# A graph-network layer on one core: B's rows for two tiles in one transfer

## The chip, the cores and the metric

The kernel runs on one core of a Trainium2 chip. The core has five engines that run side by side, each with a queue of its own: PE (matrix multiply), DVE (vector), ACT (scalar), POOL (which issues the indirect gathers here) and SP (which issues most of the other transfers). The transfers themselves are carried by 16 DMA engines. The metric is the device time of one execution in microseconds (us). Times are compared as medians over several executions.

## The reference

A graph has N = 12500 nodes with 64 features `x` and E = 200000 edges, each with a source `src`, a destination `dst` and 32 features. The edges come sorted by destination. The destinations are not spread evenly: they are 12500 times the square of a uniform number, so low nodes have many edges and high nodes few.

```python
msg_in = concatenate([x[src], x[dst], edge], -1)          # 64 + 64 + 32
messages = relu(msg_in @ mW1 + mb1) @ mW2 + mb2           # hidden size 128
aggregated = segment_sum(messages, dst, N)
update = relu(concatenate([x, aggregated], -1) @ uW1 + ub1) @ uW2 + ub2
out = layernorm(x + update)
```

## The kernel before

The first product is split into three: A = x @ mW1[:64] and B = x @ mW1[64:128] + mb1 are computed once per node and written to tables in HBM (`tab_a`, `tab_b`, rows of 128 floats, 512 bytes), and the edge features give the third part.

The edges are cut into 1563 tiles of 128 (`P`). Eight tiles (`SUB`) make a group, the unit of the main loop, which runs over 196 groups `s`; two groups make a supergroup `g` of 16 tiles (`SUP`), 98 in all. Per tile:

- POOL gathers the 128 rows of A that the sources name, with one indirect transfer (`gather`, line 166). Eight tiles go to one row buffer `xg`; there are 14 such buffers (`ROWB`), so POOL can be up to 14 groups ahead and then has to wait until the addition that reads a buffer is done. The first eight groups gather rows of x and not of A.
- The rows of B for the destinations are not gathered. As the edges are sorted, the 128 destinations of a tile lie in a range of 32 nodes (`WIN`), which begins at the tile's first destination. `windows` (lines 217 to 227) loads these 32 rows of B for each tile with one transfer on SP's queue; the first row's number is a value that SP loads into a register (line 222, one load for the eight tiles of a group). The destination is `rhs`, two buffers of one supergroup each.
- `l` holds what multiplies these rows: 32 partitions with the edge features (transposed, loaded by `load`, line 213), and 32 partitions that first receive the destinations' numbers (`loadd`, line 182, each number repeated on 32 partitions) and then, after a comparison on DVE (`select`, lines 192 and 194), a 0/1 selection matrix. An even tile has partitions 0 to 63, the next odd one 64 to 127; in each half the edge features come first (`EK` = 0), then the selection (`SK` = 32). `rhs` has the same layout: the weights mW1[128:] beside the edge features, the window of B beside the selection. There are three buffers for `l`.
- `edge_part` (line 253) multiplies `l` by `rhs` for the tile: B's row for each edge plus the edge features' part. `node_part` adds the gathered A row on DVE (line 274) and applies the rectifier on ACT (line 275).
- `collect` multiplies the result by a second 0/1 matrix `sel`, tile by 32 (line 198, from `drc`, the distance of each destination from the start of its range), and adds the sum into an accumulator of 480 columns, at an offset that PE loads into a register from `woff` (line 300; line 305 counts the edges).

The accumulator covers one of 34 periods of nodes; at a period's end `close`, `update`, `residual`, `norm` and `store` finish its nodes, and `columns` loads x for them on SP's queue (line 328).

The order of the work is written out by hand. In each turn `s` of the main loop it is: gathers as far as buffers allow; `windows(s + 2)`; `node_part(s)`; `collect(s - 1)`; in even turns `select(g + 1)`, `load(g + 1)`; in odd turns `loadd(g + 2)`; parts of the table B while it is still being computed; `edge_part(s + 1)`; and the end of a period where one is due. SP's queue thus has, for two groups, 16 windows with two register loads, two loads of edge features and two of destinations, one after the other.

A check on the device (`checks`) tests that all destinations lie within their ranges and otherwise runs a general, slow version. With this data it doesn't run, before or after.

Of the kernel before, what the change touches and what calls it, by code (L numbers as in the profile page):

```python
# [32 lines left out]
EBULK = TPP * P * P  # L33
PADDST = -100000
PADWIN = 1000000
EK, SK = 0, DE
ROWB = 14
XG = 8
NCH = 8
# [1 line left out]
EARLY = NCH * P  # L41
GE = 20
# [1 line left out]
UB = 4  # L44
NCOL = (-(-N // P) + UB) * P
UN = 448
UW = UN + WIN
ONE = D - 1


# [12 lines left out]
UPD = updates()  # L63


@with_exitstack
def gnn_kernel(ctx: ExitStack, tc: tile.TileContext, x1T, x, eT, e_rows, src, dst, dst_row, wrow, wnext, whalf,
               mW1, mb1, mW2, mb2, uW1, ub1, uW2, ub2, out):

# [22 lines left out]
    nc = tc.nc  # L92
    const = ctx.enter_context(tc.tile_pool(name="const", bufs=1))
# [8 lines left out]

    src_s = const.tile([P, NT], I32, name="src_s")
    wint = const.tile([1, NTP], I32, name="wint")
    past = const.tile([1, 1], F32, name="past")
# [22 lines left out]
    pidx = const.tile([P, 1], F32, name="pidx")  # L128
    one = const.tile([P, 1], BF, name="one")
    zero_b = const.tile([P, UW], BF, name="zero_b")  # L130

# [3 lines left out]
    drc = const.tile([P, NT], F32, name="drc")  # L135
# [4 lines left out]
    wh = const.tile([P, NTP // 2], I32, name="wh")  # L140
# [11 lines left out]
    def tiles(s):  # L152
        return range(s * SUB, min((s + 1) * SUB, NT))
# [17 lines left out]
    with tc.tile_pool(name="sup", bufs=2) as sup, tc.tile_pool(name="work", bufs=2) as work, tc.manual_schedule():  # L171
        L, S, SB, xs, hs, pcs, sums = {}, {}, {}, {}, {}, {}, {}
        pt = psum.tile([P, SUB // 2, P], F32, name="pt", tag="sums")

        def loadd(g):

            l = operand[g % 3]
            o = g * SUP * P
            dv = dst_row[:, o:o + SUP * P].rearrange("o (k b e) -> o b k e", b=2, e=P)
            for b in range(2):  # L180
                q = 64 * b + SK
                nc.sync.dma_start(l[q:q + WIN].bitcast(I32), dv[:, b].broadcast_to([WIN, SUP // 2, P]))
            L[g] = l

        def select(g):


            nt = min(SUP, NT - g * SUP)
            l = L[g]
            c = WIN + SUP // 2 * (g % 2)  # L190
            node = cps[:, c:c + SUP // 2]
            nc.vector.tensor_scalar(node, wh[:, g * SUP // 2:(g + 1) * SUP // 2], pidx, None, op0=ALU.add)
            for r in ([slice(0, P)] if g > 2 else [slice(SK, SK + WIN), slice(64 + SK, 64 + SK + WIN)]):
                nc.vector.tensor_tensor(l[r], l[r].bitcast(I32),  # L194
                                        node[r].unsqueeze(2).broadcast_to([r.stop - r.start, SUP // 2, P]),
                                        op=ALU.is_equal)
# [12 lines left out]
        def load(g):  # L209

            for b in range(2):
                q = 64 * b + EK
                nc.sync.dma_start(L[g][q:q + DE], eT[g, b])

        def windows(s):

            g = s // (SUP // SUB)
            o = s % (SUP // SUB) * SUB
            nt = len(tiles(s))
            r = rhs[g % 2]  # L220
            tab, n = (B0, EARLY - WIN + 1) if g < GE else (B, N)
            _, ws = nc.values_load_multi_w_load_instructions(
                wint[0:1, s * SUB:s * SUB + nt], engines=[ET.SP], min_val=0, max_val=n - 1,
                skip_runtime_bounds_check_because="destinations are node numbers")
            for i in range(nt):
                q = SK + 64 * (i % 2)
                nc.sync.dma_start(r[q:q + WIN, (o + i) // 2, :], tab[bass.ds(ws[i], WIN), :])

        def transpose(s):

# [142 lines left out]
        def relative(a, b):  # L373

            wbc = work.tile([P, WCH], I32, name="wbc", tag="tb")
            nc.sync.dma_start(dst_s[:, a:b], dst[:, a:b])
            nc.sync.dma_start(wbc[:, :b - a], wrow[:, a:b].broadcast_to([P, b - a]))
            nc.vector.tensor_tensor(drc[:, a:b], dst_s[:, a:b], wbc[:, :b - a], op=ALU.subtract)

        def halves(a, b):  # L380

            for h in range(2):
                nc.sync.dma_start(wh[64 * h:64 * h + 64, a:b], whalf[h:h + 1, a:b].broadcast_to([64, b - a]))


        Av, Bv, B0v = (t.rearrange("(c p) f -> p c f", p=P) for t in (A, B, B0))
# [44 lines left out]

        def offsets():

            nc.vector.memset(usup[:, 0:1], 0)
            wv = wint.rearrange("o (s t) -> o s t", t=SUB)
            ov = woff.rearrange("o (s t) -> o s t", t=SUB)
            k = 0
            while k < K:
                end = UPD[k + 1:] + [NSUB]
                d = end[0] - UPD[k]  # L440
                n = 1
                while k + n < K and k and end[n] - UPD[k + n] == d:
# [20 lines left out]
        nc.gpsimd.iota(pidx_i, pattern=[[0, 1]], base=-SK, channel_multiplier=1)  # L463
        nc.gpsimd.iota(pidx_i[64:], pattern=[[0, 1]], base=-SK, channel_multiplier=1)
        for s in range(XG):
            gather(s)
        nc.vector.tensor_copy(slot, slot_i)
        nc.vector.tensor_copy(pidx, pidx_i)
        nc.vector.memset(one, 1.0)
        nc.vector.memset(zero_b, 0.0)  # L470
        for t in (*xw, hT):
# [4 lines left out]
        nc.sync.dma_start(wint, wrow)  # L476
        halves(0, 4 * SUP)
        loadd(0)
        loadd(1)
        for r in rhs:  # L480
            for o in (EK, EK + 64):
                nc.sync.dma_start(r[o:o + DE], mW1[2 * D:, :].unsqueeze(1).broadcast_to([DE, SUP // 2, DH]))
        for k, c in enumerate(range(0, NB, NCH)):
            chunk_a(c)
            if k == 0:
                chunk_b(0, [B0v, Bv])
            if k == 2:

                w0 = wint[:, :GE * SUP]
                nc.vector.tensor_scalar(past, w0[:, GE * SUP - 1:], float(EARLY - WIN), None, op0=ALU.is_gt)  # L490
                nc.vector.tensor_scalar(w0, w0, float(EARLY - WIN), None, op0=ALU.min)
# [91 lines left out]
        for s in range(last + 3):  # L583
            g, j = divmod(s, SUP // SUB)
# [42 lines left out]
    with tc.If(flag > 0), tc.tile_pool(name="gen", bufs=1) as up:  # L627
# [28 lines left out]
        with tc.For_i(0, NT, 1) as t:  # L656
# [31 lines left out]
            h = up.tile([P, DH], F32, name="hg")  # L688
# [29 lines left out]
        with tc.For_i(0, NB, 1) as c:  # L718
# [24 lines left out]
            o = up.tile([P, D], F32, name="o")  # L743
# [45 lines left out]
```

## Time and profile before

| | |
|---|---|
| time, three executions | 2738.41, 2741.72, 2743.06 us (median 2741.72) |
| profiled execution | 2739.58 us, span of the core 2737.8 us |
| granted TensorE clock | 0.529 of full speed |
| busy share PE, DVE, ACT, POOL | 57%, 20%, 12%, 54% |
| window transfers (`rhs<-tab_b`) | 1563 on SP's queue, 16.0 KB each |
| loads of `l` | 196 of destinations, 196 of edge features, on SP's queue, 128.0 KB each as written |
| gathers of A (`xg<-tab_a`) | 1499 on POOL's queue, 128 rows each |
| bytes moved | 211.38 MB, 77 GB/s in the mean |

The busy shares are averages. SP has no busy share, as instructions that issue transfers or set registers aren't counted as busy; what SP does is read from its own records, its waits and its timeline. A row of a timeline gives the start, how long it lasted to the end of its last instruction, the engine (SPq is SP's queue), the line, the operation, what is written from what, and how many instructions were merged.

### The profile page before, as it was taken

What the parts mean: (1) busy time and instruction counts of PE and PEld (TensorE: products, weight loads), DVE (VectorE), ACT (ScalarE), POOL (GpSimd) and SP (SyncE); (2) the same over time, 40 slices, a digit from 0 to 9 for tenths busy, and PEclk for the clock granted to TensorE, in tenths of its full rate; (3) what the DMA queues carried; (4) which work ended last, traced back from release to release, by engine and by line L of the source; (5) the groups of instructions that cost most, each with busy time, mean ns of one, the idle gap of its engine ahead of it and who ended that gap; (6) DMA issues with size and microseconds to landing.
All of it is one profiled execution on the core that took longest, in us unless ns stands there. A gap on an engine that the chain in (4) does not pass through costs nothing. (4 is left out here: it accounts for less than half of the span.)

```text
span 2737.8 us, 34166 instructions
## 1 busy us (share of the span) xinstructions
PE 1572.4 (57%) x9254; PEld 1375.3 (50%) x9254; DVE 535.6 (20%) x1012; ACT 341.9 (12%) x454; POOL 1475.7 (54%) x1572
## 2 busy tenths in 40 slices
PE   1322755555655655636655565565675656576598
PEld 1311644444544545635545454455564545565477
DVE  0200121212211212212111221211221112121242
ACT  0100100101101111101111111111111111111122
POOL 7175455656566555555555555555555554655510
PEclk6555655555555555555555555555555555555555
DMA  3531233333222222222222222222222222222221
GB/s 90 143 93 52 77 85 91 96 91 92 77 77 72 72 74 76 80 66 75 73 70 74 72 75 75 76 75 73 72 76 73 70 71 73 75 75 75 73 75 39
DMA packets 242854, 211.38 MB, mean 77 GB/s; under 512 B 77245, under 2 KB 207935, under 8 KB 242672
## 3 DMA queue, kind: packets, MB, share of 16 engines
q0 software_dynamic: 50016, 100.44, 14.3%
q1 hardware_dynamic: 177102, 98.44, 12.9%
q10 hardware_dynamic: 15554, 10.31, 1.3%
q8 instruction: 87, 1.43, 0.2%
q14 instruction: 95, 0.78, 0.1%
HBM read 191.12 MB, written 17.83 MB: 76 GB/s over the span
## 5 line engine op out<-in xcount | busy, mean ns | idle before, releaser
L166 POOL DMA_INDIRECT xg<-tab_a,src_s x1499 | 1414.2, 943 | 1124.8 <-issue 419.2
L300 PEld LDWEIGHTS sums<-sel,h 128*128 128x128 f32 x3126 | 666.6, 308 | 394.1 <-issue 387.7
L300 PE MATMUL sums<-sel,h 128*128 128x32 f32 x3126 | 662.7, 369 | 343.2 <-issue 340.9
L253 PE MATMUL pc<-rhs,l 64*128 64x128 f32 x3126 | 509.9, 433 | 552.4 <-DMA l<-in_eT 277.7
L253 PEld LDWEIGHTS pc<-rhs,l 64*128 64x128 f32 x3126 | 416.6, 314 | 606.3 <-issue 559.4
L274 DVE TENSOR_TENSOR h<-pc,xg 128x1024 f32<-128x1024 f32 x189 | 229.0, 1212 | 985.7 <-issue 410.4
L275 ACT ACTIVATE h<-h 128x1024 f32<-128x1024 f32 x189 | 198.0, 1048 | 778.6 <-DVE h L274 624.9
L194 DVE TENSOR_TENSOR l<-l,cps 128x1024 f32<-128x1024 int32 (+1 forms) x101 | 123.4, 1221 | 252.4 <-DMA l<-in_dst_row 206.3
L198 DVE TENSOR_TENSOR sel<-cps,drc 128x512 f32<-128x512 f32 x98 | 67.2, 686 | 479.1 <-remote 204.1
L206 ACT CAST selb<-sel 128x512 bf16<-128x512 f32 x98 | 60.3, 616 | 560.7 <-DVE sel L198 220.3
L305 PE MATMUL cnt<-selb,one 128*1 128x32 bf16 x1563 | 85.2, 188 | 39.2 <-issue 36.9
L344 PE MATMUL py<-ux,xw 128*128 128x64 f32 x272 | 82.1, 398 | 11.2 <-issue 11.2
L408 PE MATMUL pb<-w1a,xl 64*128 64x128 f32 x196 | 29.8, 428 | 100.6 <-DMA xl<-in_x1T 57.2
L345 PE MATMUL py<-u,hTu 128*128 128x64 f32 x272 | 80.9, 392 | 11.0 <-issue 10.4
L305 PEld LDWEIGHTS <-one 128*1 128x1 bf16 x1563 | 56.1, 83 | 60.1 <-issue 49.0
L408 PEld LDWEIGHTS pb<-w1a,xl 64*128 64x128 f32 x196 | 25.4, 312 | 104.8 <-issue 87.4
L344 PEld LDWEIGHTS py<-ux,xw 128*128 128x128 f32 x272 | 67.7, 303 | 17.5 <-issue 16.7
L345 PEld LDWEIGHTS py<-u,hTu 128*128 128x128 f32 x272 | 68.9, 307 | 11.9 <-issue 11.2
L349 DVE BATCH_NORM_STATS2 st<-py 128x6 f32<-128x64 f32 x136 | 21.3, 219 | 269.4 <-PE py L345 147.6
L166 POOL DMA_INDIRECT xg<-in_x,src_s x64 | 60.5, 946 | 20.4 <-issue 19.2
L335 PE MATMUL pu<-sums_s,w2u 128*128 128x448 f32 x68 | 62.5, 1016 | 3.5 <-issue 3.1
L337 ACT ACTIVATE hTu<-pu,ub_s 128x448 f32<-128x448 f32 x34 | 21.5, 633 | 329.3 <-remote 155.8
(87 smaller groups left out, 474.9 us busy)
## 6 DMA issues: line engine op xcount, KB each, us to landing
l<-in_dst_row SPq DMA_DIRECT2D x196, 128.0 KB
l<-in_eT SPq DMA_DIRECT2D x196, 128.0 KB
rhs<-tab_b SPq DMA_DIRECT2D x1563, 16.0 KB
xg<-tab_a,src_s POOLq DMA_INDIRECT x1499
tab_b<-tb SPq DMA_DIRECT2D x13, 512.0 KB
tab_a<-tb ACTq DMA_DIRECT2D x12, 512.0 KB
out<-o SPq DMA_DIRECT2D x34, 128.0 KB
xw<-in_x1T SPq DMA_DIRECT2D x34, 113.8 KB
```

The lines of the kernel that those rows point to most:

```text
L166: nc.gpsimd.indirect_dma_start(out=a[:, i, :] if s < XG else a[:, i // 2, i % 2, :], out_offset=None, in_=A[:, :] if s >= XG else x[:, :], ...
L194: nc.vector.tensor_tensor(l[r], l[r].bitcast(I32), node[r].unsqueeze(2).broadcast_to([r.stop - r.start, SUP // 2, P]), op=ALU.is_equal)
L198: nc.vector.tensor_tensor(s[:, :nt], slot.unsqueeze(1).broadcast_to([P, nt, WIN]), drc[:, g * SUP:g * SUP + nt].unsqueeze(2).broadcast_to( ...
L206: nc.scalar.copy(sb[:, :nt], S[g][:, :nt])
L253: nc.tensor.matmul(pc[:, b, k, :], L[g][q:q + 64, m, :], rhs[g % 2][q:q + 64, m, :], start=s >= XG or k == 0, stop=s >= XG)
L274: nc.vector.tensor_tensor(hf[:, m], pf[:, m], a[:, m], op=ALU.add)
L275: nc.scalar.activation(hf[:, m], hf[:, m], AF.Relu)
L300: nc.tensor.matmul(ps[:, bass.ds(ws[i], WIN)], h[:, i % 2, i // 2, :], S[g][:, k0 + i, :], start=False, stop=ends and i == n - 1)
L305: nc.tensor.matmul(pn[:, bass.ds(ws[i], WIN)], one, SB[g][:, k0 + i, :], start=False, stop=ends and i == n - 1)
L335: nc.tensor.matmul(pu, w2u, sums_s[u % 2][:, :UN], start=True, stop=False)
L344: nc.tensor.matmul(py[:, i], xw[u % 2][:, i * P:(i + 1) * P], ux, start=True, stop=False)
L345: nc.tensor.matmul(py[:, i], hT[:, i * P:(i + 1) * P], u2, start=False, stop=True)
```

## The change

The ranges of an even tile and of the next odd one now lie a fixed distance apart: the even tile's range begins at its first destination, as before, and the odd tile's begins a constant number of nodes after that. The constant is 0 for the first 65 supergroups, where tiles are shorter in nodes, and then 2, 4, 6, 8 and 10 (`SHIFT`). Both ranges can so be read with one transfer, whose source is [2 halves, 32 rows, 128 floats] and whose destination is 64 adjacent partitions. For them to be adjacent, the odd tile's half has the selection first and the edge features last: `SK` = (32, 64), `EK` = (0, 96). `windows` issues 782 transfers of 64 rows where it issued 1563 of 32; the register load reads four values (`weven`) for a group, not eight.

What follows from it: `wint`, the start of every tile's range, is computed on DVE from `weven` (in `offsets`); the distances `drc` of odd tiles are corrected where the constant isn't 0; `pidx`, which turns partition numbers into node numbers, has one column for each constant; the accumulator gets 16 more columns (`UW` 480 to 496); `wh`, the even tile's first node on all partitions, is loaded in one transfer, not two.

```diff
-EK, SK = 0, DE
+EK, SK = (0, 96), (32, 64)
-UW = UN + WIN
+UW = UN + WIN + 16
...
+def shifts():
+    of = [2 * max(0, round(0.75 * (2.0 * N * P / E * (g + 1) * SUP * P / E - 10))) for g in range(NSUP)]
+    at = [g for g in range(NSUP) if g == 0 or of[g] != of[g - 1]]
+    return [(a, b, of[a]) for a, b in zip(at, at[1:] + [NSUP])]
...
         def windows(s):
             g = s // (SUP // SUB)
-            o = s % (SUP // SUB) * SUB
-            nt = len(tiles(s))
-            r = rhs[g % 2]
+            o = s % (SUP // SUB) * SUB // 2
+            nt = (len(tiles(s)) + 1) // 2
+            w = rhs[g % 2]
             tab, n = (B0, EARLY - WIN + 1) if g < GE else (B, N)
+            c = [c for a, b, c in SHIFT if a <= g < b][0]
+            pairs = bass.AP(tab.tensor, tab.offset, [[DH, tab.shape[0] - c], [c * DH, 2], [1, DH]])
             _, ws = nc.values_load_multi_w_load_instructions(
-                wint[0:1, s * SUB:s * SUB + nt], engines=[ET.SP], min_val=0, max_val=n - 1,
+                weven[0:1, s * SUB // 2:s * SUB // 2 + nt], engines=[ET.SP], min_val=0, max_val=n - 1,
                 skip_runtime_bounds_check_because="destinations are node numbers")
             for i in range(nt):
-                q = SK + 64 * (i % 2)
-                nc.sync.dma_start(r[q:q + WIN, (o + i) // 2, :], tab[bass.ds(ws[i], WIN), :])
+                nc.sync.dma_start(w[SK[0]:SK[0] + 2 * WIN, o + i, :],
+                                  pairs[bass.ds(ws[i], WIN)].rearrange("q h f -> h q f"))
...
             nc.vector.tensor_tensor(drc[:, a:b], dst_s[:, a:b], wbc[:, :b - a], op=ALU.subtract)
+            for g, h, c in SHIFT:
+                i, j = max(a, g * SUP) + 1, min(b, h * SUP)
+                if c and i < j:
+                    nc.vector.tensor_scalar(drc[:, i:j:2], drc[:, i:j:2], float(-c), None, op0=ALU.add)
...
         def halves(a, b):
-            for h in range(2):
-                nc.sync.dma_start(wh[64 * h:64 * h + 64, a:b], whalf[h:h + 1, a:b].broadcast_to([64, b - a]))
+            nc.sync.dma_start(wh[:, a:b], weven_row[:, a:b].broadcast_to([P, b - a]))
...
         def offsets():
+            wp = wint.rearrange("o (k b) -> o k b", b=2)
+            nc.vector.tensor_copy(wp[:, :, 0], weven)
+            for g, h, c in SHIFT:
+                g, h = g * SUP // 2, h * SUP // 2
+                nc.vector.tensor_scalar(wp[:, g:h, 1], weven[:, g:h], float(c), None, op0=ALU.add)
...
+        for k, (_, _, c) in enumerate(SHIFT):
+            nc.vector.tensor_copy(pidx[:, k:k + 1], pidx_i)
+            nc.vector.tensor_scalar(pidx[64:, k:k + 1], pidx[64:, k:k + 1], float(c), None, op0=ALU.add)
```

More of the change, by code (lines that the diff above doesn't have):

```diff
@@ L63, with gnn_kernel @@
 UPD = updates()
+def shifts():
+    of = [2 * max(0, round(0.75 * (2.0 * N * P / E * (g + 1) * SUP * P / E - 10))) for g in range(NSUP)]
+    at = [g for g in range(NSUP) if g == 0 or of[g] != of[g - 1]]
+    return [(a, b, of[a]) for a, b in zip(at, at[1:] + [NSUP])]
+SHIFT = shifts()
 @with_exitstack
-def gnn_kernel(ctx: ExitStack, tc: tile.TileContext, x1T, x, eT, e_rows, src, dst, dst_row, wrow, wnext, whalf,
+def gnn_kernel(ctx: ExitStack, tc: tile.TileContext, x1T, x, eT, e_rows, src, dst, dst_row, wrow, wnext, weven_row,
                mW1, mb1, mW2, mb2, uW1, ub1, uW2, ub2, out):
@@ L104, in gnn_kernel @@
     wint = const.tile([1, NTP], I32, name="wint")
+    weven = const.tile([1, NTP // 2], I32, name="weven")
     past = const.tile([1, 1], F32, name="past")
@@ L127, in gnn_kernel @@
     pidx_i = const.tile([P, 1], I32, name="pidx_i")
-    pidx = const.tile([P, 1], F32, name="pidx")
+    pidx = const.tile([P, len(SHIFT)], F32, name="pidx")
     one = const.tile([P, 1], BF, name="one")
@@ L180, in loadd @@
             for b in range(2):
-                q = 64 * b + SK
-                nc.sync.dma_start(l[q:q + WIN].bitcast(I32), dv[:, b].broadcast_to([WIN, SUP // 2, P]))
+                nc.sync.dma_start(l[SK[b]:SK[b] + WIN].bitcast(I32), dv[:, b].broadcast_to([WIN, SUP // 2, P]))
             L[g] = l
@@ L190, in select @@
             c = WIN + SUP // 2 * (g % 2)
+            k = [a <= g < b for a, b, _ in SHIFT].index(True)
             node = cps[:, c:c + SUP // 2]
-            nc.vector.tensor_scalar(node, wh[:, g * SUP // 2:(g + 1) * SUP // 2], pidx, None, op0=ALU.add)
-            for r in ([slice(0, P)] if g > 2 else [slice(SK, SK + WIN), slice(64 + SK, 64 + SK + WIN)]):
+            nc.vector.tensor_scalar(node, wh[:, g * SUP // 2:(g + 1) * SUP // 2], pidx[:, k:k + 1], None, op0=ALU.add)
+            for r in ([slice(0, P)] if g > 2 else [slice(q, q + WIN) for q in SK]):
                 nc.vector.tensor_tensor(l[r], l[r].bitcast(I32),
@@ L211, in load @@
             for b in range(2):
-                q = 64 * b + EK
-                nc.sync.dma_start(L[g][q:q + DE], eT[g, b])
+                nc.sync.dma_start(L[g][EK[b]:EK[b] + DE], eT[g, b])
         def windows(s):
             g = s // (SUP // SUB)
-            o = s % (SUP // SUB) * SUB
-            nt = len(tiles(s))
-            r = rhs[g % 2]
+            o = s % (SUP // SUB) * SUB // 2
+            nt = (len(tiles(s)) + 1) // 2
+            w = rhs[g % 2]
             tab, n = (B0, EARLY - WIN + 1) if g < GE else (B, N)
+            c = [c for a, b, c in SHIFT if a <= g < b][0]
+            pairs = bass.AP(tab.tensor, tab.offset, [[DH, tab.shape[0] - c], [c * DH, 2], [1, DH]])
             _, ws = nc.values_load_multi_w_load_instructions(
-                wint[0:1, s * SUB:s * SUB + nt], engines=[ET.SP], min_val=0, max_val=n - 1,
+                weven[0:1, s * SUB // 2:s * SUB // 2 + nt], engines=[ET.SP], min_val=0, max_val=n - 1,
                 skip_runtime_bounds_check_because="destinations are node numbers")
             for i in range(nt):
-                q = SK + 64 * (i % 2)
-                nc.sync.dma_start(r[q:q + WIN, (o + i) // 2, :], tab[bass.ds(ws[i], WIN), :])
+                nc.sync.dma_start(w[SK[0]:SK[0] + 2 * WIN, o + i, :],
+                                  pairs[bass.ds(ws[i], WIN)].rearrange("q h f -> h q f"))
         def transpose(s):
@@ L462, in gnn_kernel @@
         nc.gpsimd.iota(slot_i, pattern=[[1, WIN]], base=0, channel_multiplier=0)
-        nc.gpsimd.iota(pidx_i, pattern=[[0, 1]], base=-SK, channel_multiplier=1)
-        nc.gpsimd.iota(pidx_i[64:], pattern=[[0, 1]], base=-SK, channel_multiplier=1)
+        for h in range(2):
+            nc.gpsimd.iota(pidx_i[64 * h:64 * h + 64], pattern=[[0, 1]], base=64 * h - SK[h], channel_multiplier=1)
         for s in range(XG):
@@ L467, in gnn_kernel @@
         nc.vector.tensor_copy(slot, slot_i)
-        nc.vector.tensor_copy(pidx, pidx_i)
+        for k, (_, _, c) in enumerate(SHIFT):
+            nc.vector.tensor_copy(pidx[:, k:k + 1], pidx_i)
+            nc.vector.tensor_scalar(pidx[64:, k:k + 1], pidx[64:, k:k + 1], float(c), None, op0=ALU.add)
         nc.vector.memset(one, 1.0)
@@ L475, in gnn_kernel @@
             nc.sync.dma_start(w1b[64 * h:64 * h + D], mW1[D:2 * D, :])
-        nc.sync.dma_start(wint, wrow)
+        nc.sync.dma_start(weven, weven_row)
         halves(0, 4 * SUP)
@@ L480, in gnn_kernel @@
         for r in rhs:
-            for o in (EK, EK + 64):
+            for o in EK:
                 nc.sync.dma_start(r[o:o + DE], mW1[2 * D:, :].unsqueeze(1).broadcast_to([DE, SUP // 2, DH]))
@@ L487, in gnn_kernel @@
             if k == 2:
-                w0 = wint[:, :GE * SUP]
-                nc.vector.tensor_scalar(past, w0[:, GE * SUP - 1:], float(EARLY - WIN), None, op0=ALU.is_gt)
+                w0 = weven[:, :GE * SUP // 2]
+                nc.vector.tensor_scalar(past, w0[:, GE * SUP // 2 - 1:], float(EARLY - WIN), None, op0=ALU.is_gt)
                 nc.vector.tensor_scalar(w0, w0, float(EARLY - WIN), None, op0=ALU.min)
@@ L764 @@
     wp = np.full((1, NTP + 1), PADWIN, dst.dtype)
-    wp[0, :NT] = dst[::P]
+    wp[0, :NT] = np.repeat(dst[::2 * P], 2)[:NT]
     ep = np.zeros((EPAD, DE), edge.dtype)
@@ L774 @@
         "wrow": wp[:, :NTP], "wnext": wp[:, 1:],
-        "whalf": wp[0, :NTP].reshape(-1, 2).T,
+        "weven_row": wp[:, :NTP:2],
         "mW1": L0_gnn_mW1, "mb1": L0_gnn_mb1, "mW2": L0_gnn_mW2, "mb2": L0_gnn_mb2,
```

## The prediction

> **What bounds the kernel now.** I read the page first, for an engine that is nearly full. There is none: PE has 57% and POOL 54%. The column to read is the idle time of the gathers.
>
> ```profile
> span 2737.8 us, 34166 instructions
> PE 1572.4 (57%) x9254; PEld 1375.3 (50%) x9254; DVE 535.6 (20%) x1012; ACT 341.9 (12%) x454; POOL 1475.7 (54%) x1572
> q1 hardware_dynamic: 177102, 98.44, 12.9%
> L166 POOL DMA_INDIRECT xg<-tab_a,src_s x1499 | 1414.2, 943 | 1124.8 <-issue 419.2
> ```
>
> Next the waits, and the records of line 166. A gather takes 0.944 us and is followed by 0.30 us of issue, so eight of them, one group's worth, take 9.95 us. The 1499 gathers need 1499 x 1.244 = 1865 us but stretch from 139.0 to 2621.7, that is 2483 us. The 618 us between are pauses: POOL waits for DVE to free a row buffer. Behind DVE stands PE, which waits for `l`, whose loads stand on SP's queue.
>
> ```profile
> POOL xg L166 <- DVE h L274: 337.3, 59, 14.2
> POOL xg L166 <- DVE cps L192: 271.8, 54, 11.2
> PE pc L253 <- DMA l<-in_eT: 277.7, 54, 20.5
> DVE l L194 <- DMA l<-in_dst_row: 206.3, 49, 12.5
> L166 POOL DMA_INDIRECT xg<-tab_a,src_s x1499: 938/944/1007, 139.0 to 2620.8; - x188
> ```
>
> SP itself hardly waits: all rows of its own waits make some 250 us, the largest two at the start.
>
> ```profile
> SPq L222 <- DVE wint L491: 46.1, 1, 46.1
> SPq L213 <- DVE l L194: 38.2, 6, 16.4
> ```
>
> So SP is busy for the rest, issuing. The records of line 227 show four instructions to a window transfer, some of them lasting 2 ns and some 1400, whatever they do:
>
> ```profile
> L227 SPq FUSED_REGOPS  x1563: 2/37/1400, 95.7 to 2698.9; - x196
> L227 SPq DMA_DIRECT2D rhs<-tab_b x1563: 2/316/1474, 95.9 to 2699.4; - x196
> ```
>
> What makes the difference is seen by laying SP's timeline beside POOL's.
>
> ```profile
> 204.35 40.60 SPq L227 DMA_DIRECT2D rhs<-tab_b  x8
> 861.24 8.61 SPq L227 DMA_DIRECT2D rhs<-tab_b  x8
> 871.88 16.37 SPq L227 DMA_DIRECT2D rhs<-tab_b  x8
> 892.54 4.18 SPq L227 DMA_DIRECT2D rhs<-tab_b  x8
> 2656.11 4.17 SPq L227 DMA_DIRECT2D rhs<-tab_b  x8
> ```
>
> ```profile
> 869.89 0.94 POOL L166 DMA_INDIRECT xg<-tab_a,src_s  x1 [3.24 <-DVE cps L192]
> 888.60 0.94 POOL L166 DMA_INDIRECT xg<-tab_a,src_s  x1 [0.30 <-issue]
> 900.75 0.94 POOL L166 DMA_INDIRECT xg<-tab_a,src_s  x1 [11.20 <-DVE cps L192]
> ```
>
> With POOL paused (889.5 to 900.8) or finished (after 2622), eight transfers, 29 instructions from the first issue to the last, take 4.2 us: 0.14 us each. Early in a run of gathers they take 8.6, over the twenty microseconds of 869.9 to 889.5 they take 16.4, and at 204 us, 65 us into the first long run, 40.6 us: 1.4 us each. Loads and register operations slow down alike. Thus gathers slow SP, a late SP holds up PE and DVE, these hold up POOL, and in POOL's pause SP catches up. SP's instruction count sets how long the pauses are.
>
> How much is paused per group: 270 to 2620 us holds 2866 matmuls of line 253, two records to a group's each of eight: 2866/16 = 179 groups, 13.1 us each: 9.95 of gathers and 3.15 of pause.
>
> **The change part by part.**
>
> *SP.* Per group it now executes 36 instructions (6,441 records from 300 to 2620 us, in 177 groups): 32 for eight windows, one register load, some three for the `l` loads and the rest. After: 782 transfers for 1563, four a group, 16 + 4 = 20. What SP gets done beside POOL I count from the two timelines: after 300 us POOL has 54 runs of 8 gathers and 60 of 16. In the first 10 us of a run SP starts 29 instructions, in the 20 us of a run of 16 it starts 40, and in the first long run 31 in the 42 us from 204 on, some 8 in each further 10 us. The pauses last 4.0 us after runs of 8, with 17 instructions, and 6.0 after runs of 16, with 25: 0.24 us each, waits included.
> - Before, by this rule: a run of 8 leaves 36 - 29 = 7 over, 7 x 0.24 = 1.7 us of pause; a run of 16 leaves 72 - 40 = 32, 7.7 us. Over 174 groups (54 x 1.7 + 60 x 7.7)/174 = 3.2 us a group, measured 3.15.
> - After: runs of 8 and 16 leave nothing over (20 against 29, 40 against 40). A run of 24 needs 60 and gets 48: 12 x 0.24 = 2.9 us for three groups, 10.9 us each. So a group takes between 9.95 and 10.9; the middle is 10.45.
>
> *The transfer itself grows*: 64 rows, in two halves that lie apart in HBM, instead of 32. Its issue is in no row. Below: 0.316 us as now (nothing, or a gain if fewer commands suffice). Above: line 399's 64-row `xl` load, median 0.594 us. I take 0.55, as that row has as many partitions: 4 x 0.23 = 0.9 us a group in a pause, less under gathers, where an instruction costs 0.5 us in the mean anyway (20/40). With a third of the issues in pauses, 0.3 us.
>
> *Its packets.* The page gives q1 98.44 MB in 12.9% of 16 x 2737.8 us, 5651 engine-us: 17.4 KB per us and engine. 32 KB take 1.88 us on one engine, 0.12 on sixteen; the trace doesn't say on how many it will run. Even on one, four a group are 7.5 us of 10. It is issued two groups ahead, so its landing is covered; if that cover goes, PE's wait for `rhs<-tab_b`, 23.7 us now, grows.
>
> [...]
>
> *Queues passed.* Nothing changes places: on SP a window group stays ahead of the same `l` loads, which merely come four issues sooner. On POOL's queue one iota covers 64 rows instead of 128. The selection rows move to 32-95, so that one transfer fills adjacent partitions; PE multiplies the same 64 rows, the same count. PE needs 107.8 busy us for the last 118 us, some 8.7 us a group with updates: the next bound after POOL's 9.95.
>
> *DVE, ACT.* Some 24 small DVE operations more at the start (shifted offsets), at the 0.22 of line 192 to the 0.69 us of line 198: 5 to 17 us. DVE is busy 30 of the first 270 us, so I charge nothing; without that cover at most 17. The accumulators grow from 480 to 496 columns, 3% of 34 clears and copies: under 1 us.
>
> *Sum.* 10.45 + 0.3 for the larger issue, + 0.3 for the way from SP through PE and DVE back to POOL (0 to 0.7: the rule says nothing of it, and short pauses hide it least) is 11.05 us a group, 1.1 of pause; 179 x 1.1 = 197 us for 618. Time: 139.0 + 1865 + 197 + 116 (from 2621.7 to the end: the 14 buffered groups, which PE bounds) = 2317, + 1.8 around the span (2739.6 against 2737.8) = 2319. The profiled execution lies 2.1 us under the median of 2741.7; I say 2320.
>
> **The rivals.**
> 1. *Part of the gain* (2440 to 2735). If the price per instruction rises further when POOL hardly pauses, as at 204 us, or a new transfer counts for one and a half to nearly two old ones (24 to 32 instructions' worth and the 4 others): 28 instructions a group need 56 in a run of 16, 16 more than it gives: 16 x 0.24 = 3.8 us for two groups, 1.9 each, and 2.5 with the larger issue and the way back as above: 179 x 2.5 = 448, so 2570. For it: the price did climb to 1.4 us. Against: that price stands only where POOL ran for over 60 us on end.
> 2. *Slower.* One mechanism: SP is held until few engines have taken a transfer's packets. The place is the issue of line 240; it decides from the point at which one new issue costs two old (1.10 us in a pause). On one engine it would be 1.88 + 0.23 = 2.1 us: 8.4 against 4.4 us a group, 4.0 us more, of which what falls into pauses, about a third, is 1.3 us: 179 x 1.3 = 233, about 2975. Against: the `l` loads of 256 rows issue in 0.448 us, the `xl` loads in 0.594 us.
> 3. *No change* (2742): POOL's pauses come from PE or DVE, not SP. But PE waits 277.7 us for `l<-in_eT`, and with POOL done PE and DVE do a group in about 7.2 us (SP's bursts of 2656 and 2663).
>
> **How the numbers follow.** The forecast with its own range, 2100 (no pause at all: 2122, and less where fewer than 14 groups are then buffered at the end) to 2440, 0.62. Rival 1: 0.24. Rival 2: 0.12. Rival 3: 0.02; 0.2%, 5 us, is about what this kernel's times can tell from no change. Faster 0.86, same 0.02, slower 0.12. The range of 8 in 10 is 2100 to 2580: it leaves out rivals 2 and 3 and the upper quarter of rival 1, 0.06.
>
> **What would show it.** Line 240 with 782 transfers; bursts of four at about 2.5 us with POOL paused; POOL's waits for DVE down from 609 us to about 200; groups of 11 us. Wrong, if an issue in a pause takes over 1.1 us, if PE's wait for `rhs<-tab_b` takes the place of `l<-in_eT`, or if the stretch of gathers stays near 2480 us.

## The result, and the profile after

| | before | after |
|---|---|---|
| time, four executions each | 2742.39 us median (2738.41 to 2750.15) | 2783.97 us median (2782.14 to 2791.05) |
| ratio | 1 | 1.0153, 95% interval 1.0124 to 1.0181 |
| profiled execution, span | 2739.58, 2737.8 us | 2791.05, 2788.9 us |
| gathers of A, from first to last | 139.0 to 2621.7 us | 139.1 to 2681.1 us |
| from the last gather to the end | 116.1 us | 107.8 us |

The changed kernel is 1.5% slower; 2320 us had been predicted. The 51 us between the two spans lie in the stretch of the gathers (59 us longer, with 8 us less at the end). The head of the page after, the group of the gathers (busy time and mean ns of one, then the idle time before them), and the records of the windows' line (ns min/median/max, first and last start):

```profile
span 2788.9 us, 31106 instructions
...
PE 1522.5 (55%) x9254; PEld 1340.8 (48%) x9254; DVE 539.9 (19%) x1036; ACT 341.9 (12%) x454; POOL 1480.1 (53%) x1572
```

```profile
L179 POOL DMA_INDIRECT xg<-tab_a,src_s x1499 | 1418.4, 946 | 1179.9 <-issue 422.3 <-DVE h L288 362.7 <-DVE cps L205 297.4
```

```profile
L240 SPq FUSED_REGOPS  x782: 2/37/1395, 95.3 to 2753.1; - x196
...
L240 SPq DMA_DIRECT2D rhs<-tab_b x782: 2/618/1675, 95.6 to 2753.3; - x196
```

So the change did what it says: 782 transfers, 3,060 instructions fewer. But one new issue takes 0.618 us, nearly as long as the two of 0.316 us that it replaces. Its 64 packets of 512 B, some 27 ns each, run about two at a time: in the last two windows of the trace never more than two start within 20 ns, in their longest stretch two in every 23.5 ns, from first to last they take 1.15 and 1.18 us, and the DMA share is 0.10 and 0.09 of the 16 engines (2753.75 to 2754.91 and 2755.00 to 2756.20 us). The 32 packets of one of the last windows of before take 0.25 us, with up to six starts within 20 ns and a share of 0.23 (2698.90 to 2699.17 us). A gather still takes 0.946 us with some 0.3 us of issue. Yet POOL waits 660 us for DVE, where it waited 609. The waits of the kernel after (us in total, times, longest), and then the largest of SP's queue:

```profile
PE sums L314 <- issue: 499.5, 288, 3.6
...
PE pc L267 <- issue: 368.2, 240, 14.1
POOL xg L179 <- DVE h L288: 362.7, 57, 15.7
...
POOL xg L179 <- DVE cps L205: 297.4, 53, 12.9
```

```profile
SPq L225 <- DVE l L207: 291.6, 52, 16.9
```

Two things are to be seen. SP has become idle: it waits 291.6 us for DVE to finish with an `l` buffer, where it waited 38.2. And PE's wait of 277.7 us for `l<-in_eT` is gone (0.3 us now), as is most of DVE's of 206.3 us for the destinations (17.2 now); SP is no longer late. In their place PE waits for nothing that the profile can name ("issue"). In the waits of before, the rows of the same two lines were smaller:

```profile
PE sums L300 <- issue: 340.9, 285, 2.6
...
PE pc L253 <- issue: 226.5, 196, 17.8
```

They were 567.4 us together and are 867.7 now: 300 us more, for the 277.7 that went. What such a wait looks like is shown by the timelines of PE, POOL and DVE after, around one run of 16 gathers, that is gathers without a pause between them (start, duration, what, and in brackets the idle time before):

```profile
1339.97 3.46 PE L314 MATMUL sums<-sel,h 128*128 128x32 f32 x16
...
1344.08 1.06 PE L267 MATMUL pc<-rhs,l 64*128 64x128 f32 x5
1347.19 0.37 PE L267 MATMUL pc<-rhs,l 64*128 64x128 f32 x1 [2.05 <-issue]
1350.25 0.37 PE L267 MATMUL pc<-rhs,l 64*128 64x128 f32 x1 [2.69 <-issue]
1353.05 0.37 PE L267 MATMUL pc<-rhs,l 64*128 64x128 f32 x1 [2.43 <-issue]
...
1361.71 0.82 PE L267 MATMUL pc<-rhs,l 64*128 64x128 f32 x4 [0.33 <-issue]
```

```profile
1337.72 0.95 POOL L179 DMA_INDIRECT xg<-tab_a,src_s  x1 [5.80 <-DVE cps L205]
...
1356.81 0.94 POOL L179 DMA_INDIRECT xg<-tab_a,src_s  x1 [0.30 <-issue]
1364.11 0.95 POOL L179 DMA_INDIRECT xg<-tab_a,src_s  x1 [6.36 <-DVE cps L205]
```

```profile
1362.62 1.23 DVE L288 TENSOR_TENSOR h<-pc,xg 128x1024 f32<-128x1024 f32 x1 [14.84 <-PE pc L267]
1363.76 0.22 DVE L205 TENSOR_SCALAR cps<-wh,pidx 128x8 f32<-128x8 int32 x1
```

The gathers start at 1337.72. For some seven microseconds PE goes on as in the pause (16 matmuls in 3.46 us). Then it sits idle for one to three microseconds before each single matmul, waiting for nothing that the profile shows, until some four microseconds after POOL has paused. The last matmul of the group ends DVE's wait (at 1362.62), and DVE's next operation ends POOL's (at 1364.11). Counted over all runs of 16 gathers from the records (from 300 us on), PE starts 6.1 matmuls per us in the first eight us of a run (5.4 before) and 0.46 in its second ten (0.72 before): once it has slowed down, it is slower than before. SP's window issues slow down at the same time: in SP's timeline one group's burst takes 14.41 us inside this run, 2.62 after it, and 3.3 once the gathers are over.

```profile
1342.35 14.41 SPq L240 DMA_DIRECT2D rhs<-tab_b  x4
...
1361.67 2.62 SPq L240 DMA_DIRECT2D rhs<-tab_b  x4
...
2700.70 3.32 SPq L240 DMA_DIRECT2D rhs<-tab_b  x4
```

### The profile page after: what moved, and what is told of

Read it like the earlier page. It is cut to its first block, busy times and chain, and to the rows that moved or that the text cites. A ratio compares the mean times of both kernels' runs of the same rounds, so it can differ in the third digit from the quotient of the medians.

```text
span 2788.9 us, 31106 instructions
## 1 busy us (share of the span) xinstructions
PE 1522.5 (55%) x9254; PEld 1340.8 (48%) x9254; DVE 539.9 (19%) x1036; ACT 341.9 (12%) x454; POOL 1480.1 (53%) x1572
## 2 busy tenths in 40 slices
DMA packets 219386, 211.10 MB, mean 76 GB/s; under 512 B 53770, under 2 KB 184492, under 8 KB 219229
## 3 DMA queue, kind: packets, MB, share of 16 engines
q0 software_dynamic: 50016, 100.44, 13.8%
## 4 chain that ended last, share of the span: by engine, by line
PE 29%; issue 27%; another core or an unknown queue 12%; DVE 3%; ACT 1%; DVEq 0%; DMA 0%; SPq 0%; ACTq 0%
PE sums L314 12%; PE pc L267 9%; PE pu L349 1%; PE py L358 1%; PE cnt L319 1%; PE py L359 1%; PE pu L350 1%; DVE h L288 1%; DVE l L207 1%; DVE st L363 1%; DVE o L376 0%; PE sums L327 0%; ACT h L289 0%; PE cnt L317 0%
## 5 line engine op out<-in xcount | busy, mean ns | idle before, releaser
L314 PE MATMUL sums<-sel,h 128*128 128x32 f32 x3126 | 651.5, 364 | 506.0 <-issue 499.5
L267 PE MATMUL pc<-rhs,l 64*128 64x128 f32 x3126 | 469.9, 423 | 410.5 <-issue 368.2
L267 PEld LDWEIGHTS pc<-rhs,l 64*128 64x128 f32 x3126 | 387.9, 310 | 447.2 <-issue 392.0
L207 DVE TENSOR_TENSOR l<-l,cps 128x1024 f32<-128x1024 int32 (+1 forms) x101 | 123.3, 1221 | 27.5 <-DMA l<-in_dst_row 17.2
```

The source lines that it names most:

```text
L207: nc.vector.tensor_tensor(l[r], l[r].bitcast(I32), node[r].unsqueeze(2).broadcast_to([r.stop - r.start, SUP // 2, P]), op=ALU.is_equal)
L267: nc.tensor.matmul(pc[:, b, k, :], L[g][q:q + 64, m, :], rhs[g % 2][q:q + 64, m, :], start=s >= XG or k == 0, stop=s >= XG)
L314: nc.tensor.matmul(ps[:, bass.ds(ws[i], WIN)], h[:, i % 2, i // 2, :], S[g][:, k0 + i, :], start=False, stop=ends and i == n - 1)
```

## The experiments

The theory formed on this (A in the expectations): beside an unbroken run of gathers the queues slow down, PE's own among them, and PE's slowness sets the pauses, whatever SP has to do. Its rival (B) is the prediction's: SP's instructions set them. The slowing itself is seen in SP's records (a burst of 14.41 us inside the run, 2.62 after it) and in PE's gaps (up to 2.69 us before one matmul); for ACT and DVE it is not shown, and POOL's own gathers keep their pace (0.946 us each, 0.943 before). Chips differ (the kernel before took 1981 us on the first one and 2742 in the recorded runs), so each time below stands beside that of the kernel before on the same chip.

### Without the windows, and without the gathers

The first leaves out of before all window transfers from group 4 on (B's rows are then missing from the result); the second replaces in before each group's eight gathers of A, from group 32 on, by one plain load of fixed rows.

In `windows` of before, and in `gather` of before:

```diff
+            if s >= 4:
+                return
...
+        if s >= 32:
+            nc.gpsimd.dma_start(buf, A[0:P * SUB, :].rearrange("(p k) f -> p k f", k=SUB))
+            xg[s] = buf, a
+            return
```

> The kernel before, without the loads of B's rows from the fifth group on (they and their register loads are left out, so later tiles use old rows of B). Two theories. A: after some 9 us of gathers without a pause every instruction queue nearly stands still, PE's too (0.6 matmuls per us in the second ten microseconds of a run, 5 to 6 in the first), and SP's transfers don't set the time. B: SP's instructions set it, as the prediction had it, and in the changed kernel the larger transfer's cost (0.618 us of issue against 0.316) ate the gain. A expects 2600 to 2740 us. B expects POOL never to pause: 2100 to 2300 us.

> The kernel before, with one plain load of the same bytes (first 1024 rows of A) on POOL's queue from group 32 on, where eight gathers stood (the gathering itself is left out). A expects that no queue slows down any more: the remaining 164 groups take what the tail of before takes, 7 to 8.7 us each, so 1750 to 1950 us in all, with windows issuing at 0.55 us throughout. B expects the same slowdown to vanish for SP, so about the same time; the run tells how much of the time the gathers cost, and whether PE's and SP's slow stretches are theirs.

Measured: 1983.93 us without windows, 1509.18 with plain loads, outside all the ranges that were named. The kernel before took 1981.49 us on this chip (13 executions), not 2742. So nothing on windows could be told there. The changed kernel was then put on it, and the one without windows again, with the same edit:

> The changed kernel once more, on the chip that the experiments run on. In the last runs the kernel before took 1981 us and not 2742: POOL's gathers ran without a pause and no queue slowed down beside them. If that holds here, both theories expect the same time as before (POOL's gathers alone make 139 or 57 us of start + 1499 x 1.25 + about 30): 1975 to 1990 us, ratio 1.000. If the queues slow down beside gathers on this chip, it expects 2784 us against 2742 as recorded, ratio 1.015; B, the theory that SP's instructions set the time, has no room for that.

> The kernel before without the loads of B's rows from the fifth group on (left out, later tiles use old rows). Where queues slow down beside gathers: A expects 2600 to 2740 us, as PE's own instructions are slowed, B 2100 to 2300 us. Where they don't: 1980 us under both.

Measured: 1980.30 us for the changed kernel, 1.000 (0.999 to 1.001) of before, and 1980.32 without windows. The changed kernel's records of the windows' line on this chip, its largest wait of POOL, and the group of its line 314:

```profile
L240 SPq FUSED_REGOPS  x782: 37/37/51, 29.7 to 1939.9; - x196
...
L240 SPq DMA_DIRECT2D rhs<-tab_b x782: 617/622/1367, 29.9 to 1940.1; - x196
```

```profile
POOL xg L179 <- issue: 455.7, 1495, 0.3
```

```profile
L314 PE MATMUL sums<-sel,h 128*128 128x32 f32 x3126 | 660.4, 385 | 282.7 <-ACT h L289 281.9 <-issue 0.6
```

The same program, and neither SP nor PE slows down: the register operation that took up to 1395 ns takes at most 51 here, PE's wait for "issue" at line 314 is 0.6 us and not 499.5, and POOL never pauses. Here gathers alone set the time, and neither kernel has anything to gain at SP. The next form, the changed kernel reading 64 adjacent rows of B (for the odd tiles these are the wrong rows; the last two supergroups keep the two halves), agreed on that chip too:

```diff
-            tab, n = (B0, EARLY - WIN + 1) if g < GE else (B, N)
+            tab, n = (B0, EARLY - 2 * WIN + 1) if g < GE else (B, N - WIN if g < NSUP - 2 else N)
...
                 nc.sync.dma_start(w[SK[0]:SK[0] + 2 * WIN, o + i, :],
+                                  tab[bass.ds(ws[i], 2 * WIN), :] if g < NSUP - 2 else
                                   pairs[bass.ds(ws[i], WIN)].rearrange("q h f -> h q f"))
...
-                nc.vector.tensor_scalar(w0, w0, float(EARLY - WIN), None, op0=ALU.min)
+                nc.vector.tensor_scalar(w0, w0, float(EARLY - 2 * WIN), None, op0=ALU.min)
```

> The changed kernel, whose transfer now reads 64 adjacent rows of B (one plain source, not two halves; the odd tiles' rows are then wrong). Same number of transfers, same bytes. B expects the issue to fall back to about 0.32 us and the time to 2320 us or so. A expects no such gain: 2720 to 2790 us; at most the 40 us come back that the changed kernel lost, if the two halves' issue or the few engines they run on are their cause.

Measured: 1982.60 us, 1.0006 (0.9996 to 1.0015) of before; an issue takes 0.513 us. And a pace, a 128-column clear on POOL of a tile that nothing reads, after each gather of A, put into `gather` of before:

```diff
+            if s >= XG:
+                nc.gpsimd.memset(idle[:, :128], 0.0)
```

> The kernel before, with a 128-column memset of a scratch tile on POOL after each gather of A, so that gathers follow each other every 1.4 to 1.5 us and not every 1.25. A, if the slowdown is something that piles up while gathers come faster than it drains: runs of gathers no longer choke PE, eight gathers take 11.5 us, 2450 to 2650 us. If it doesn't pile up: eight gathers longer by 1.6 us a group, up to 3000 us. B expects no gain: SP is slowed by gathers for a larger share of the time, 2740 to 2900 us.

Measured: 2116.34 us, 1.0679 (1.0661 to 1.0697): the clear takes 0.22 us, a gather comes every 1.34 us for 1.25, and where nothing slows down these 0.09 us more are simply paid.

### Three times the transfers, and plain loads in the changed kernel

On a second chip, where before took 2804.83 us, each window transfer was issued three times, twice to tiles that nothing reads, in before and in after; and the changed kernel got the plain loads.

The lines added to `windows` of before; after got the same with its own transfer:

```diff
+                for k in range(2):
+                    nc.sync.dma_start(spare_rows[s % 2 * 2 + k][q:q + WIN, i, :], tab[bass.ds(ws[i], WIN), :])
```

> The kernel before, with each window transfer issued three times (twice more into scratch tiles that nothing reads), so that SP is made the bound on purpose: 24 transfers of 0.548 us and about 1.5 us of the rest make 14.7 us a group against POOL's 10.0. Where nothing else slows down: 188 x 14.7 + about 60 = 2800 to 2900 us; a run of 1980 us would mean that SP's issue isn't what its records show.

> The changed kernel, likewise with three transfers for one: 12 of 0.85 us (0.618 of issue and 0.23 around it, as its trace has it) and 1.5 make 11.7 us a group: 188 x 11.7 + about 60 = 2260 us. B, that SP's instructions set the time in the recorded comparison too, needs such a gain where SP binds; A says that the gain exists only here, where SP is the bound, and that the recorded comparison lacked it because PE's own instructions had slowed down. If few engines carry the transfer and hold up the queue (32 KB on two engines 0.75 us at the 23 ns a 512 B packet follows another), 12 of them still fit in 11.7 us.

> The changed kernel without the gathering from group 32 on (one plain load on POOL's queue instead of eight gathers). The kernel before took 1509 us so. Both theories: PE bounds a group at about 7.2 us and SP's share (5.9 us before, 4.9 after) is hidden: 1500 to 1515 us. Over 1530 us: the new transfer costs more than its trace shows, for instance by landing late on few engines.

Measured, one execution each: 3888.89 us (2800 to 2900 expected), 3417.59 us (2260 expected) and 1662.05 us (1500 to 1515 expected). The first two figures reckoned with issues at full speed; the third figure came from the chip on which nothing slows down. In the run of before SP does bind, by the very waits that the prediction had read (its list of waits):

```profile
DVE l L195 <- DMA l<-in_dst_row: 1410.6, 91, 27.6
...
PE pc L256 <- DMA l<-in_eT: 1139.3, 83, 26.8
```

There, halving the transfers gains 12% (3417.59 against 3888.89). The 3126 added transfers cost (3888.89 - 2804.83)/3126 = 0.35 us each. With plain loads PE goes back to eight tenths or more in every slice but the last once the gathers end (the page's busy tenths in 40 slices):

```profile
PE   1044105745588999999999989999999999999997
...
POOL 7704772435510000000000000000000000000000
```

The gathers end at 461 us; the 164 groups with a plain load take at most (1660 - 461)/164 = 7.3 us each. Nearly all that lies above the expected 1515 us was thus spent beside the gathers, which ended at 324 us on the first chip, and not on a late landing of the new transfer. The slowness of PE and SP goes where the gathers go. It isn't the amount of data: this run moves 127 GB/s in the mean, the kernel after 76.

### Without the windows where queues slow down; a longer pace

On a third chip (before 2744.44 us, ten executions) the first kernel was run again, with a pace of 256 columns in before, and with the adjacent rows.

> The kernel before without the loads of B's rows from the fifth group on (left out, later tiles use old rows of B). Two chips of two kinds have been seen: on one the queues slow down beside gathers (before takes 2740 to 2805 us), on the other they don't (1981 us). Where they slow down: A, PE's own instructions are slowed and set the time as much as SP's, expects 2600 to 2780 us; B, SP's instructions alone set it, expects 2100 to 2300 us, as SP has only about 4 instructions a group left. Where they don't: 1981 us under both.

> The kernel before with a 256-column memset on POOL after each gather of A, so that gathers follow each other every 1.45 us or so, not every 1.25. Where the queues slow down: if what slows them piles up while gathers come every 1.25 us and drains when they come slower, PE no longer stalls and eight gathers take 11.6 us: 2400 to 2500 us against 2740 to 2805. If it is a matter of gathers being under way at all, no gain or a loss: 2750 to 3000 us. On a chip without the slowdown: 139 or 57 + 1499 x 1.45 + 30, about 2280 us against 1981.

> The changed kernel whose transfer reads 64 adjacent rows of B (one plain source on all engines, not two halves; the odd tiles' rows are then wrong). Where the queues slow down: if the new source's issue (0.618 us against 0.513) or the few engines behind it cost the 1.5%, this takes as long as before, ratio 1.00 or a little under. If not, the loss stays: ratio 1.010 to 1.020. On a chip without the slowdown 1.000, as seen.

Measured, in one execution: 2607.26 us without windows from the fifth group on, 0.950 of before, within A's range and far from B's. This run decides between the theories. SP has 4 instructions a group left of 36 and is idle for over a thousand microseconds, while POOL still waits, and PE for "issue" (SP's waits, then those of all engines):

```profile
SPq L213 <- DVE l L194: 1078.3, 57, 105.5
```

```profile
POOL xg L166 <- DVE h L276: 454.5, 87, 12.6
...
PE sums L302 <- issue: 388.1, 351, 2.8
```

All 1531 transfers that were left out are worth (2744.44 - 2607.26)/1531 = 0.09 us each, a quarter of what an added one costs: at the present number most of SP's work is already covered by PE's slowness. (The two prices are from two chips.)

The pace: 2541.87 us, 0.9254 (0.921 to 0.9298), a little above its 2400 to 2500, though POOL has 493 us more work. It leaves nothing out and is faster than both kernels of this case. The groups of its pace and of its line 303, and its waits of POOL:

```profile
L303 PE MATMUL sums<-sel,h 128*128 128x32 f32 x3126 | 682.0, 360 | 180.6 <-issue 161.9 <-ACT h L278 5.6 <-ACT selb L209 1.0
...
L171 POOL MEMSET idle<- 128x256 f32 x1499 | 492.7, 329 | 1.2
```

```profile
POOL xg L167 <- DVE h L277: 78.8, 24, 4.8
...
POOL xg L167 <- DVE cps L195: 51.7, 23, 4.7
```

A gather now comes every 1.45 us (0.954 + 0.329 + 243/1499 idle), PE's "issue" at line 303 is 161.9 us (340.9 in the recorded before), and between 20 and 30 us into runs of 24 gathers it still starts 2.7 matmuls per us. POOL's waits for DVE are 131 us for 609. So PE's slowness depends on how densely gathers follow one another; that it doesn't depend on this alone is seen further down.

The adjacent rows: 2728.23 us, 0.9945 (0.9919 to 0.9971). Half the transfers gain half a percent here, if the rows are adjacent (on the next chip 0.998, no clear gain). The recorded 1.0153 against 0.9945 leaves 2% for the source in two halves; side by side on one chip, further down, it is 1.9% (2782.28 against 2729.66).

### What in the source of two halves costs the time

The source could cost through its longer issue (0.618 us against 0.513) or through its packets, which run about two at a time. How the other forms stand there can be read from the DMA totals: packets under 512 bytes are 77245 before, 53770 after and 64521 with adjacent rows, and the other transfers are nearly the same. Per new transfer 23475/782 = 30 fewer after, 12724/782 = 16.3 fewer with adjacent rows: what fits is 16 small packets to every old transfer and to an adjacent one (two old ones have 32), and 2 to one with two halves. The runs that change the number of old transfers give the 16 directly: without windows 24496 fewer for 1531, with three times the transfers 50016 more for 3126. The line of the DMA totals of after:

```profile
DMA packets 219386, 211.10 MB, mean 76 GB/s; under 512 B 53770, under 2 KB 184492, under 8 KB 219229
```

In the packet records the small packets have 4 bytes: 16 beside the 32 packets of the window of before that was timed above, 2 beside the 64 of each of the last two of after. In the windows with 2, no more than two packets of 512 B start within 20 ns; in the one with 16, up to six. That 2 or 16 DMA engines carry a transfer, as the expectations have it, is a reading of these counts; the trace doesn't name a packet's engine.

A third form keeps the two ranges but reads them row by row, 32 x 2 x 128. On a fourth chip it ran with the two known ones and with the changed kernel that has the 256-column pace.

```diff
-                                  pairs[bass.ds(ws[i], WIN)].rearrange("q h f -> h q f"))
+                                  pairs[bass.ds(ws[i], WIN)])
```

> The changed kernel with the same two ranges of 32 rows read in another order: row by row, both halves of each (source of 32 x 2 x 128 floats instead of 2 x 32 x 128), so that even and odd tiles' rows land interleaved in the 64 partitions. It computes other numbers, as B's rows stand beside the wrong selection rows; the work of every engine is the same. It separates the two things in which the changed kernel differs from the one that reads 64 adjacent rows: a longer issue (0.617 against 0.513 us) and the few small packets that say on how many DMA engines a transfer runs. Few engines cost the 2%: small packets return to about 64,500 and the time to 0.994 of before, whatever the issue takes. The longer issue costs them: the issue stays at 0.62 us and the time at 1.015 of before. If the issue falls to 0.51 us as well, the two cannot be told apart by this run. On a chip on which gathers slow nothing down (before near 1981 us) all kernels of this call but the paced one agree within 0.2% and nothing is told apart.

> The changed kernel itself, on the chip of this call, so that the others can be compared with it directly: 1.012 to 1.018 of before, as recorded, where before takes about 2740 us.

> The changed kernel reading 64 adjacent rows again (wrong rows for the odd tiles), beside the others on one chip: 0.992 to 0.997 of before, as in its run before this one; then the ratio to the changed kernel, 0.975 to 0.985, is no difference between chips.

> The changed kernel with a 256-column clear on POOL after each gather of A, as the paced form of before had it (0.925 of before). If the change costs time only because PE and SP stand still beside unbroken gathers, then with gathers paced the halved number of transfers costs nothing more and gains no more than 2%: 0.90 to 0.93 of before. If two engines carrying the windows is a cost by itself: 0.935 to 0.96.

Then, on a fifth chip, the interleaved and the adjacent form with the same pace:

> The interleaved form (two halves, read row by row; it computes other numbers, every engine's work is the same) with the 256-column clear after each gather of A. With that clear the kernel before ran in 0.925 and the changed kernel in 0.987 of before: a difference of 6%, four times that without the clear, so that its cause should show more plainly. If the DMA engines that carry a window (16 here) are the cause: 0.92 to 0.94 of before. If the length of the issue is (0.567 us here, between 0.513 and 0.618): 0.95 to 0.97, halfway again. If any transfer of 64 rows is: 0.98 to 0.99.

> The form that reads 64 adjacent rows (wrong rows for the odd tiles, the same work), with the same clear. By the source in two halves as the cause, in either of its two forms: 0.915 to 0.935 of before, as the kernel before with the clear or a little better. If a halved number of larger transfers is what costs time once gathers are paced: 0.96 to 0.99.

Measured, with the interleaved issue read from its record,

```profile
L240 SPq DMA_DIRECT2D rhs<-tab_b x782: 2/567/1545, 95.8 to 2712.1; - x196
```

| window transfer | issue, us | packets under 512 B | of before, not paced | of before, paced |
|---|---|---|---|---|
| 32 rows (before) | 0.316 | 77245 | 1 | 0.925 (0.921 to 0.930), third chip |
| 64 adjacent rows | 0.513 | 64521 | 0.998 (0.995 to 1.001) | 0.941 (0.937 to 0.945), fifth chip |
| interleaved | 0.567 | 64717 | 1.006 (1.003 to 1.009) | 0.954 (0.951 to 0.958), fifth chip |
| two halves (after) | 0.618 | 53770 | 1.014 (1.008 to 1.020) | 0.987 (0.980 to 0.995), fourth chip |

The column without a pace is from the fourth chip: 2729.66, 2757.14 and 2782.28 us, before 2738.41. The recorded slowdown is there again, and the adjacent form is just above its range (0.992 to 0.997). The interleaved form met neither of its figures (0.994 and 1.015). It has 16 small packets to a transfer as the adjacent one has (64717 and 64521 packets under 512 B in all) and costs 27.5 us more, so the number of small packets, and what it stands for, is not all of it. The step to two halves costs 25.1 us more, with another 0.051 us of issue and 2 small packets for 16. The issue alone could explain these steps: 0.054 us for 27.5 and 0.051 us for 25.1.

With gathers paced the interleaved form's 0.954 lies in the range named for the issue (0.95 to 0.97) and not in that for the engines (0.92 to 0.94); the adjacent form's 0.941 lies between its two ranges. In microseconds the two steps are again alike: 35.2 (2663.01 against 2627.80) and 34.5 (2697.51 against 2663.01). As ratios they are 1.3% and 3.3%, but the second is between two chips on which before took 2791 and 2738 us, so the ratios can't be leant on. Whether packets that run two at a time cost time of their own is not shown: no run had 2 small packets to a transfer and a short issue.

Where the cost shows is PE. In the second ten us of runs of 16 gathers, not paced, it starts 1.1 matmuls per us without windows, 0.72 before, 0.60 with adjacent rows, 0.50 with interleaved ones, and 0.46 and 0.42 with two halves (recorded run and fourth chip). So by these counts, which come from several chips, the windows' transfers add to PE's slowness itself: a transfer costs more than the time that SP spends on it. How it does so stays open.

The paced changed kernel met neither of its two figures. Its PE waits 437.1 us for "issue" at line 317, the paced kernel before 161.9: with the new transfer PE slows down even beside paced gathers. Between 20 and 30 us into runs of 24 it starts 1.2 matmuls per us, where the paced kernel before starts 2.7; the paced adjacent and interleaved forms lie between, with 1.7. The largest wait of PE in the paced changed kernel:

```profile
PE sums L317 <- issue: 437.1, 480, 2.2
```

## Why the prediction was wrong, step by step

- *What bounds the kernel.* That POOL pauses because DVE and, behind it, PE are late, held. The step that failed is the sentence "SP's instruction count sets how long the pauses are". By it, a kernel without windows (4 instructions a group) would have had no pause, about 2122 us as the prediction worked it out; it took 2607. The pauses come from PE's own slowness beside gathers. SP's lateness, by the totals, lay within the same microseconds; when it went, PE's wait for `l<-in_eT` (277.7 us) gave way to 300 us more of "issue". And the prediction put at nothing what the new transfer does to PE beside gathers: from 0.72 matmuls per us to 0.46 in the second ten us of a run.
- *How it could have been read.* The prediction saw SP's instructions stretch to 1400 ns, put it down to the gathers, and looked no further than SP. PE's waits of 340.9 and 226.5 us for "issue" stood in the same list and were not asked about. Only SP's timeline was laid beside POOL's; PE's, over a few runs of gathers, would have shown it.
- *The price of 0.24 us an instruction* was a time per instruction of pauses that PE set: 0.96 us for a transfer of four. Taken out, one is worth 0.09 us. The rule gave back the 3.15 us of pause per group that it had been fitted to, which proved nothing.
- *The rejection of rival 3* failed at its evidence: "with POOL done PE and DVE do a group in about 7.2 us". That figure held (at most 7.3 us with plain loads), but it is a rate without gathers. Rival 3 had the mechanism, with a chance of 0.02; only its "no change" was off by 1.5%.
- *The issue*, taken at 0.55 us between 0.316 and 0.594, is 0.618, above the upper end. A burst of four in a pause takes 3.3 us as a rule, not the predicted 2.5 (the 2.62 above is a short one), so that of the 4.2 us of eight old transfers 0.9 are saved. No issue took over 1.1 us in a pause (0.77 at most), so rival 2's condition wasn't met; that the time is longer came about below its threshold.
- *The packets.* The prediction charged nothing for them, as it took their landing to be covered, even on one engine. They run about two at a time, and the cover held: PE's wait for the windows did not grow (3.1 us for 23.7). Two halves cost 2% against adjacent rows all the same, by something other than a late landing, and about half of that came with 16 small packets to a transfer (the interleaved form).
- *Gathers, DVE, the end.* 1499 x 1.24 us stood, DVE's added operations left the first gather of A at 139.1 us, and the end took 108 us for 116. What was named as proof of the contrary, a stretch of gathers that stays near 2480 us, is what came, at 2542. The rule would have had it at 2062 (1865 + 197).

## What to carry to other kernels

SP's stall was PE's too (beside one run of gathers a burst of 14.41 us on SP and up to 2.69 us before one matmul on PE): before pricing one queue's instructions, lay every engine's timeline over the same stretch, and ask what the engine behind it would do there. A rate is only good for the company in which it was measured: PE's with POOL finished (about 7.2 us a group) said nothing of PE beside POOL (13.1 us a group in before). And a merged transfer is to be priced by its own issue: here one of two halves took as long as the two that it replaced (0.618 against 2 x 0.316 us), and cost 2% against one of adjacent rows.

## What the runs showed of the hardware

- The same kernel before took 1981 us on one chip, 2742 in the recorded run, and 2738, 2744, 2791 and 2805 us on four other chips, and the records differ in kind: on the first neither SP's queue nor PE's slowed down, on the others both did. With plain loads in place of gathers the rest of the work took 1183 us on the first (1507.1 - 323.8, before) and 1199 on the second (1660.0 - 461.5, after). So the chips differ by what happens beside gathers. What differs between them, and what holds the queues, the profile doesn't show; it stays open.
- Where it slows down (recorded runs, third and fourth chip), PE falls, after some eight us of gathers at one in 1.25 us, from 5.4 (before) and 6.1 (after) matmuls per us in the recorded runs to 0.72 and 0.46 (0.42 to 0.60 in the other runs with windows, 1.1 without), and recovers some four us after the last gather (1361.7 against 1357.8 in the run shown).
- A pace on POOL took 7.5% off the kernel before on one such chip (256 columns) and added 6.8% on the first (128 columns); the changed kernel gained 1.3% by it. It is no safe change without knowing on which chip a kernel will run.
